# Attention: ScalarE instead of VectorE empties the bank of softmax denominators

## The chip, the cores and the metric

The kernel runs on one core of one Trainium2 chip. That core has a matrix engine (TensorE, "PE" in the profile, with its weight loads as "PEld"), VectorE ("DVE"), ScalarE ("ACT"), GpSimd ("POOL"), a queue engine for transfers ("SP"), and 16 DMA engines. The metric is the device time of one execution in microseconds (us); less is better.

## The reference, cut to what matters

The model is one image of 256 channels and 64x64 pixels. It passes a linear-attention layer on the image, then a self-attention over its 4096 pixels as tokens, then a mixture of eight experts. Only the self-attention matters here: 8 heads of 32 channels, softmax over 4096 keys, scale 256 to the power -0.5.

```python
def _L1_attn_ref(x, w_qkv, b_qkv, w_out, b_out):      # x: 1 x 4096 x 256
    qkv = x @ w_qkv + b_qkv
    q, k, v = split into 8 heads of 32
    dots = jnp.einsum('bhid,bhjd->bhij', q, k) * scale
    attn = jax.nn.softmax(dots, axis=-1)
    out = jnp.einsum('bhij,bhjd->bhid', attn, v)
    return out @ w_out + b_out
...
t = t + _L1_attn_ref(_ln_t(t), ...)
```

## The kernel before

The work is in float32. Before the loop, queries and keys lie with channels on the partitions (`qk`) and the values with tokens on the partitions (`v`). A measured bound on the scores lets the kernel leave out the subtraction of the row maximum, so each softmax is the plain exponential over its sum.

**Rounds and steps.** A round is one chunk of 512 queries (`qc`, eight of them) and one group of four heads (`g`, two of them): 16 rounds. A round has 32 steps, one for each tile of 128 keys. All 512 steps are written out in order by the list `places`, and each engine runs its own instructions in the order written, except where `tc.issue_after(x)` holds one behind instruction `x` in its engine's order.

**One step.** `scores(r, i)` multiplies 128 keys by 512 queries for four heads (L1074). Head 0 goes to the bank `one`, of which there is a single one; heads 1 to 3 go to a group of three banks, `three`, of which there are two in turn. ScalarE takes the exponential of `one` (L1082, 512 columns) and then of `three` (L1084, 1536 columns) into a weights buffer. Two steps later `value_sums` multiplies the weights by the values into the bank `acc` (L1033). So TensorE's order in the loop is: scores of step i, value products of step i - 2, scores of step i + 1, and so on.

**Denominators.** The sum of the weights over the keys is gathered in buffers: `add` (L1100, VectorE, 128x2048) adds most steps' weights to the round's total; every fourth step's are added by an accumulating DMA that GpSimd issues (L1089). At step 5 of the next round `gather` adds the two totals (L1120). At step 9 `pack` sums the total over the partitions by products with ones, into the first bank of a `three` group (`den`, L1033 again), and copies that bank to `rec` (L1129). The SP queue then writes four rows of `rec` to memory and reads them back spread over 128 partitions (L1131, L1132). At step 17 `turn` takes the reciprocal and brings it back to all channels; at step 29 `spread` multiplies the round's result (L1149). Rounds 1 to 15 do this for the round before, so `pack` runs 15 times; the last round has an ending of its own, whose copy of `acc` ScalarE makes (L1112).

**The banks around `pack`.** Since `den` takes a turn of the two `three` groups, the turns near step 9 are: step 8 the first group, step 9 the second, `den` the first, step 10 the second, step 11 the first. So step 10 waits until ScalarE has read step 9's scores, one step earlier than usual; and the scores of step 11 cannot begin until L1129 has emptied `den`. In VectorE's order L1129 stands behind an `add`.

In odd rounds from the third on, steps 13 and 25 also hold two tiles of the output projection (L1011, with VectorE's L1015 to empty it), in one `three` group.

Of the kernel before, what the change touches and what calls it, by code (L numbers as in the profile page):

```python
# [25 lines left out]
AF = mybir.ActivationFunctionType  # L26
# [5 lines left out]
C = 256  # L32
# [3 lines left out]
CH = 512  # L36
# [75 lines left out]
def tile_conv_attn_hybrid(ctx: ExitStack, tc: tile.TileContext, a: dict, out: bass.AP):  # L112
    nc = tc.nc
# [29 lines left out]
    def chunk(i):  # L143
        return slice(CH * i, CH * (i + 1))
# [41 lines left out]
    with ExitStack() as phase:  # L186
# [397 lines left out]
        def packed(jobs):  # L584

            steps = []
            for job in jobs:
                if not steps or sum(j[0] for j in steps[-1]) + job[0] > CH:
                    steps.append([])
                steps[-1].append(job)  # L590
            return steps
# [247 lines left out]
    with ExitStack() as phase:  # L839
# [179 lines left out]
        with tc.If(tame > 0) as branch:  # L1019
            with (  # L1020
# [6 lines left out]
                def three_banks():  # L1027
                    return ps.tile([P, 3, CH], F32, tag="three", name="ps_three", bufs=2)
# [26 lines left out]
                head = lambda z, hd: z[:, CH * hd : CH * (hd + 1)]  # L1055
# [1 line left out]

                rounds = [(qc, g) for qc in range(NCH) for g in range(KC)]
                places = [(r, i) for r in range(len(rounds)) for i in range(NT)]
                weights_of, acc_of, sums_of = {}, {}, {}  # L1060

                def scores(r, i):
                    qc, g = rounds[r]
                    step = NT * r + i
                    n = min(free)[1]
                    free.remove(min(free))
                    pe = buffers[n]
                    one = ps.tile([P, CH], F32, tag="one", name="ps_one")
                    three = three_banks()
                    for hd in (1, 2, 3, 0):  # L1070
                        hs = slice(D * hd, D * (hd + 1))
                        to = three[:, hd - 1] if hd else one
                        for u in range(2):
                            nc.tensor.matmul(  # L1074
                                to[CELL * u : CELL * (u + 1), :],
                                qk[hs, 1, g, P * i + CELL * u : P * i + CELL * (u + 1)],
                                qk[hs, 0, g, chunk(qc)],
                                start=True,
                                stop=True,
                                skip_group_check=True,  # L1080
                            )
                    first = nc.scalar.activation(head(pe, 0), one, AF.Exp, scale=C**-0.5)  # L1082
                    with tc.issue_after(first.ins):
                        nc.scalar.activation(pe[:, CH:], three.rearrange("p h n -> p (h n)"), AF.Exp, scale=C**-0.5)  # L1084
                    weights_of[r, i] = pe
                    if i in (own, other):
                        sums_of[r, i] = n
                    elif moved(r, i):
                        nc.gpsimd.dma_start(buffers[sums_of[r, other]], pe, accum_op=ALU.add)  # L1089
                        free.append((step + 6, n))  # L1090
                    else:
                        free.append((step + 3, n))

                def moved(r, i):
                    return i in by_dma and (r < last or i < NT - 8)
# [18 lines left out]
                def by_ones(to, weights, start, stop):  # L1114
                    per_head(to, lambda hd: ones, lambda hd: head(weights, hd), start, stop)
# [9 lines left out]
                def pack(r):  # L1125
                    den = three_banks()[:, 0]
                    by_ones(den, buffers[sums_of[r, own]], True, True)
                    rec = work.tile([P, CH], F32, tag="rec", name="rec")
                    nc.vector.tensor_copy(rec, den)  # L1129
                    some = work.tile([P, CH // D], F32, name="some")  # L1130
                    nc.sync.dma_start(dens, rec[::D, :])  # L1131
                    nc.sync.dma_start(some, packed(dens))  # L1132
                    held.append(some)
                    free.append((NT * (r + 1) + 11, sums_of[r, own]))
# [25 lines left out]
                for s, (r, i) in enumerate(places):  # L1160
                    qc, g = rounds[r]
                    scores(r, i)
                    if s > 1:
                        value_sums(*places[s - 2])
                        if places[s - 2][1] == NT - 1:
                            take(places[s - 2][0], nc.vector.tensor_copy)
                    if r and i == 5:
                        gather(r - 1)
                    if r and i == 9:
                        pack(r - 1)  # L1170
                    if r and i == 17:
                        turn()
                    if r and i == 29:
                        spread(r - 1)
                    if qc and g == KC - 1 and i in (13, 25):
                        some_projections(2)
                    if s < len(places) - 2:
                        add(r, i)

                den = three_banks()[:, 0]  # L1180
# [5 lines left out]
                rec = work.tile([P, CH], F32, tag="rec", name="rec")  # L1186
# [6 lines left out]
        with branch.Else():  # L1193


            with (
# [8 lines left out]
                for hd in range(2 * 4):  # L1205
                    g, hs = hd // 4, slice(D * (hd % 4), D * (hd % 4 + 1))
                    nc.vector.tensor_copy(ka[:D, :], qk[hs, 1, g, :])
                    for qc in range(NCH):
# [16 lines left out]
                        for i in range(NT):  # L1225
                            sc = ps.tile([P, CH], F32, tag="sc", name="ps_sc")
                            nc.tensor.matmul(sc, ka[:, tok(i)], qa, start=True, stop=True)
                            pe = work.tile([P, CH], F32, name="pe1")
# [10 lines left out]
                        rec = bigb.tile([D, CH], F32, name="rec1")  # L1239
# [10 lines left out]
    with ExitStack() as phase:  # L1250
# [15 lines left out]
        def each(name):  # L1266
            return small.tile([P, NT, NE], F32, name=name)

        def one(name):
            return small.tile([P, NT], F32, name=name)  # L1270
# [30 lines left out]
        with ExitStack() as routing:  # L1301
# [41 lines left out]
            for n in range(2):  # L1343
                first, hot, place = each(f"first{n}"), each(f"hot{n}"), one(f"place{n}")
# [295 lines left out]
```

## Time and profile before

| What | Value |
|---|---|
| median of three runs | 2819.03 us (2815.43 to 2820.85) |
| the profiled execution's own time | 2818.95 us |
| its span, first to last instruction | 2817.1 us |
| the 512 steps of attention | from 1115.6 to 2220.6 us of the span |
| TensorE busy, 1200 to 2220 us | 1011.5 of 1020 us |
| ScalarE busy, 1200 to 2220 us | 916.1 of 1020 us |
| VectorE busy, 1200 to 2220 us | 866.0 of 1020 us |
| one L1129 (VectorE, 128x512 out of a bank) | 683 ns, 15 times |
| one L1082, one L1084 (ScalarE) | 598 and 1445 ns, 512 times each |
| one L1100 (VectorE, 128x2048) | 2.29 us |

In the timeline a line gives start, duration, engine, source line, operation, and in brackets how long the engine stood idle before it and whose end released it. The ends of matrix products are modelled, so their starts are the surer figure. A step's length is best read from one L1082 to the next.

### The profile page before, as it was taken

What the parts mean: (1) busy time and instruction counts of PE and PEld (TensorE: products, weight loads), DVE (VectorE), ACT (ScalarE), POOL (GpSimd) and SP (SyncE); (2) the same over time, 40 slices, a digit from 0 to 9 for tenths busy, and PEclk for the clock granted to TensorE, in tenths of its full rate; (3) what the DMA queues carried; (4) which work ended last, traced back from release to release, by engine and by line L of the source; (5) the groups of instructions that cost most, each with busy time, mean ns of one, the idle gap of its engine ahead of it and who ended that gap; (6) DMA issues with size and microseconds to landing.
All of it is one profiled execution on the core that took longest, in us unless ns stands there. A gap on an engine that the chain in (4) does not pass through costs nothing. (4 is left out here: it accounts for less than half of the span.)

```text
span 2817.1 us, 71992 instructions
## 1 busy us (share of the span) xinstructions
PE 2668.2 (95%) x31078; PEld 1218.8 (43%) x31078; DVE 1888.8 (67%) x2491; ACT 1483.1 (53%) x2045; POOL 812.5 (29%) x914
## 2 busy tenths in 40 slices
PE   6889999988999989999999999999999689999996
PEld 5454336735434654111212121212222168888884
DVE  6758788575878886888888888888888721111114
ACT  3232323222232312999898989898988732222222
POOL 2067778205777731000000000000000022222220
PEclk9999999999999999999999999999999879999997
DMA  5000000000000000555555555555555356666665
GB/s 142 6 23 28 7 31 17 8 0 26 27 9 30 15 21 1 106 116 119 109 111 110 117 108 119 109 111 110 112 108 119 85 182 221 192 200 195 205 216 189
DMA packets 120043, 264.97 MB, mean 94 GB/s; under 512 B 20098, under 2 KB 81128, under 8 KB 105636
## 3 DMA queue, kind: packets, MB, share of 16 engines
q0 software_dynamic: 22368, 133.18, 22.2%
q1 hardware_dynamic: 90168, 118.15, 13.0%
q10 hardware_dynamic: 7180, 8.93, 0.9%
q8 instruction: 248, 4.06, 0.6%
q14 instruction: 79, 0.65, 0.1%
HBM read 126.76 MB, written 18.12 MB: 51 GB/s over the span
## 5 line engine op out<-in xcount | busy, mean ns | idle before, releaser
L1074 PE MATMUL ps_three<-qk 32*64 32x512 f32 x6144 | 566.6, 616 | 10.3 <-DVE rec L1129 7.3
L1074 PE MATMUL ps_one<-qk 32*64 32x512 f32 x2048 | 560.0, 616 | 0.6 <-ACT pe L1082 0.6
L1100 DVE TENSOR_TENSOR act<-act,pe 128x2048 f32<-128x2048 f32 x195 | 446.8, 2291 | 89.8 <-ACT pe L1084 55.2
L564 ACT COPY sm<-ps_sc 128x384 f32<-128x384 f32 (+3 forms) x454 | 218.5, 511 | 529.4 <-PE ps_sc L738 345.6
L1084 ACT ACTIVATE pe<-ps_three 128x1536 f32<-128x1536 f32 x330 | 476.9, 1445 | 0.0
L568 DVE TENSOR_TENSOR sm<-ps_sc,mask 128x512 f32<-128x512 f32 (+3 forms) x740 | 340.1, 519 | 69.9 <-PE ps_sc L738 66.8
L1100 DVE TENSOR_TENSOR act<-act 128x2048 f32<-128x2048 f32 x150 | 343.8, 2292 | 60.6 <-ACT act L1084 48.9
L568 POOL TENSOR_TENSOR sm<-sm,mask 128x192 f32<-128x192 f32 (+3 forms) x428 | 349.8, 848 | 111.9 <-ACT sm L564 111.5
L1089 POOL DMA_DIRECT2D pe<-pe x108 | 92.9, 860 | 961.7 <-ACT pe L1084 660.2
L1033 PE MATMUL ps_acc<-pe,v 128*32 128x512 f32 x2640 | 353.2, 607 | 0.0
L1549 ACT ACTIVATE hid<-ps_hp,cols 128x256 f32<-128x256 f32 (+1 forms) x288 | 133.1, 462 | 360.1 <-PE ps_hp L1546 346.3
L1074 PEld LDWEIGHTS ps_three<-qk 32*64 32x64 f32 x6144 | 113.2, 130 | 425.8 <-ACT pe L1082 232.2
L1084 ACT ACTIVATE act<-ps_three 128x1536 f32<-128x1536 f32 x182 | 263.2, 1446 | 0.0
L1546 PE MATMUL ps_hp<-xe,w 128*128 128x256 f32 (+1 forms) x1152 | 246.8, 371 | 0.0
L1555 PE MATMUL ps_yp<-w,hid 128*128 128x256 f32 x1088 | 240.8, 379 | 0.0
L1082 ACT ACTIVATE pe<-ps_one 128x512 f32<-128x512 f32 x330 | 197.3, 598 | 69.2 <-PE ps_one L1074 45.6
L738 PE MATMUL ps_sc<-qk 32*64 32x384 f32 (+3 forms) x3584 | 232.4, 458 | 0.0
L568 POOL TENSOR_TENSOR sm<-sm,ycut 128x384 f32<-128x384 f32 (+4 forms) x146 | 147.3, 1030 | 250.6 <-ACT sm L564 250.3
L1546 PEld LDWEIGHTS ps_hp<-xe,w 128*128 128x128 f32 x1152 | 201.2, 190 | 39.4 <-ACT hid L1549 5.3
L1555 PEld LDWEIGHTS ps_yp<-w,hid 128*128 128x128 f32 x1088 | 204.2, 190 | 26.4
L754 PE MATMUL ps_acc<-sm,v 128*32 128x256 f32 (+3 forms) x2688 | 213.2, 419 | 0.1
L1525 DVE TENSOR_SCALAR xe<-ps_tp,cols 128x256 f32<-128x256 f32 (+1 forms) x72 | 34.8, 525 | 239.3 <-PE ps_tp L1521 217.1
(253 smaller groups left out, 3009.8 us busy)
## 6 DMA issues: line engine op xcount, KB each, us to landing
pe<-pe POOLq DMA_DIRECT2D x108, 1024.0 KB
w<-in_L_ffn_W SPq DMA_DIRECT2D x72, 1024.0 KB
by<-recs SPq DMA_DIRECT2D x48, 256.0 KB
b<-in_L_ffn_b SPq DMA_DIRECT2D x36, 128.0 KB
rows<-in_x SPq DMA_DIRECT2D x16, 256.0 KB
zrows<-act SPq DMA_DIRECT2D x4, 1024.0 KB
y<-yrows ACTq DMA_DIRECT2D x8, 512.0 KB
y<-yrows SPq DMA_DIRECT2D x8, 512.0 KB
```

The lines of the kernel that those rows point to most:

```text
L564: nc.scalar.copy(sm[:, :used], sc[:, :used])
L568: done = engine.tensor_mul(to, of, mk.unsqueeze(1).to_broadcast(list(to.shape)))
L738: nc.tensor.matmul(scs[h][u : u + rows, at : at + n], kT[hs[h], P * i + u : P * i + u + rows], qT[hs[h], CH * ix + CELL * c0 : CH * ix + C ...
L754: nc.tensor.matmul(acc[hs[h], CELL * c0 : CELL * c1], v[:, i, hs[h]], sms[h][:, at : at + n], start=not begun[0], stop=last and at == plac ...
L1033: nc.tensor.matmul(to[D * hd : D * (hd + 1), :], lhsT(hd), rhs(hd), start=start, stop=stop, skip_group_check=True,)
L1074: nc.tensor.matmul(to[CELL * u : CELL * (u + 1), :], qk[hs, 1, g, P * i + CELL * u : P * i + CELL * (u + 1)], qk[hs, 0, g, chunk(qc)], sta ...
L1082: first = nc.scalar.activation(head(pe, 0), one, AF.Exp, scale=C**-0.5)
L1084: nc.scalar.activation(pe[:, CH:], three.rearrange("p h n -> p (h n)"), AF.Exp, scale=C**-0.5)
L1100: latest[:] = [nc.vector.tensor_add(total, total, weights_of[r, i]).ins]
L1546: nc.tensor.matmul(hp[:, :n], w1[:, k, tok(m)], x_now[:, k, :n], start=k == 0, stop=k == KC - 1)
L1549: nc.scalar.activation(hid[:, m, :n], hp[:, :n], AF.Gelu, bias=cols[:, m : m + 1])
L1555: nc.tensor.matmul(yp, hid[:, m, tok(j)], w2[:, m, :], start=m == 0, stop=m == NH - 1)
```

## The change

The copy of `den` to `rec` is made by ScalarE. A list `emptied` holds the ScalarE instruction behind which the next one has to stand. The copy is put behind L1084 of step 9, and the first exponential of step 10 is put behind the copy. Nothing else moves: the lists of instructions of TensorE, GpSimd and SP are the same in both kernels, VectorE's lacks 15 copies and ScalarE's has 15 more, each between L1084 of step 9 and L1082 of step 10. The product that first writes `den`'s bank again and the transfer of `rec` now wait for ScalarE instead of VectorE.

```diff
-                weights_of, acc_of, sums_of = {}, {}, {}
+                weights_of, acc_of, sums_of, emptied = {}, {}, {}, []
...
-                    first = nc.scalar.activation(head(pe, 0), one, AF.Exp, scale=C**-0.5)
+                    with tc.issue_after(emptied[-1]) if emptied else nullcontext():
+                        first = nc.scalar.activation(head(pe, 0), one, AF.Exp, scale=C**-0.5)
                     with tc.issue_after(first.ins):
-                        nc.scalar.activation(pe[:, CH:], three.rearrange("p h n -> p (h n)"), AF.Exp, scale=C**-0.5)
+                        emptied[:] = [
+                            nc.scalar.activation(
+                                pe[:, CH:], three.rearrange("p h n -> p (h n)"), AF.Exp, scale=C**-0.5
+                            ).ins
+                        ]
...
                     rec = work.tile([P, CH], F32, tag="rec", name="rec")
-                    nc.vector.tensor_copy(rec, den)
+                    with tc.issue_after(emptied[0]):
+                        emptied.append(nc.scalar.copy(rec, den).ins)
```

## The prediction

> **What bounds the kernel now.** I read the shares of busy time first, then the windows of the attention stage, then who waited for whom in that stage, then the timeline of one `pack`.
>
> ```profile
> 1200.00:2220.00 1020.00, 1011.52 (x11568) 211.31 (x11572) 866.04 (x500) 916.07 (x945) 87.73 (x102) 1.00 0.54 111
> ```
>
> The columns are PE, PEld, DVE, ACT, POOL, the granted clock, the DMA share and GB/s. In these 1020 us TensorE is busy for 1011.5, at full clock; ScalarE for 916 (90%), VectorE for 866 (85%). So this stage ends when TensorE is through, and only time that TensorE loses here counts. What does it lose, and to whom?
>
> ```profile
> PE ps_three L1074 <- DVE rec L1129: 7.3, 15, 0.5
> PE ps_three L1074 <- DVE t L1015: 1.2, 1, 1.2
> ```
>
> These are all the waits of TensorE in that window: 15 times some 0.5 us for the copy that the change moves, 7.3 us in all, and one 1.2 us for a projection's bank. Nothing else. Round 1's `pack` shows how one of the fifteen comes about:
>
> ```profile
> 1203.01 1.07 PE L1033 MATMUL ps_acc<-act,v 128*32 128x512 f32 x8
> 1203.78 1.45 ACT L1084 ACTIVATE pe<-ps_three 128x1536 f32<-128x1536 f32 x1
> 1203.89 1.04 PE L1033 MATMUL ps_three<-pe,ones 128*32 128x512 f32 x8
> ...
> 1204.97 2.29 DVE L1100 TENSOR_TENSOR act<-act,pe 128x2048 f32<-128x2048 f32 x1
> ...
> 1205.28 0.68 PE L1074 MATMUL ps_three<-qk 32*64 32x512 f32 x6
> ...
> 1205.81 0.59 PE L1074 MATMUL ps_one<-qk 32*64 32x512 f32 x1
> ...
> 1206.32 1.06 PE L1033 MATMUL ps_acc<-pe,v 128*32 128x512 f32 x8
> 1206.54 0.60 ACT L1082 ACTIVATE act<-ps_one 128x512 f32<-128x512 f32 x1 [1.31 <-PE ps_one L1074]
> 1207.03 1.45 ACT L1084 ACTIVATE act<-ps_three 128x1536 f32<-128x1536 f32 x1
> 1207.17 0.69 DVE L1129 COPY rec<-ps_three 128x512 f32<-128x512 f32 x1
> ...
> 1207.91 0.68 PE L1074 MATMUL ps_three<-qk 32*64 32x512 f32 x6 [0.53 <-DVE rec L1129]
> ...
> 1209.19 0.60 ACT L1082 ACTIVATE act<-ps_one 128x512 f32<-128x512 f32 x1 [0.71 <-PE ps_one L1074]
> ...
> 1211.23 0.60 ACT L1082 ACTIVATE pe<-ps_one 128x512 f32<-128x512 f32 x1
> ```
>
> L1084 at 1203.78 is step 9's. `den` is written by 1204.93 (1203.89 + 1.04), but VectorE has just begun an `add` that runs to 1207.26; the copy follows and ends at 1207.86, and step 11's scores start at 1207.91. Meanwhile ScalarE stands idle for 1.31 us ahead of step 10's first exponential at 1206.54, and 0.71 us ahead of step 11's at 1209.19. After that a step takes 2.04 us again (1209.19 to 1211.23).
>
> **The change, part by part.**
>
> *The new copy.* The nearest row is the only ScalarE copy of this form in the attention stage:
>
> ```profile
> L1112 ACT COPY act<-ps_acc x1: 586/586/586, 2223.0 to 2223.0; 128x512 f32<-128x512 f32 x1
> ```
>
> It ran behind exponentials with no table load before it; copies of 128x512 elsewhere on ScalarE take 586 to 618 ns. In the changed program's list, too, no table load is added. The copy names up to six things to wait for (the `den` products and five transfers of the round before). The transfers have long landed, and the semaphore instructions ahead of L1082 take 17 ns each, so five cost 0.09 us at most. In round 1, ScalarE is free at 1205.23, 0.30 after `den` is written. A ScalarE instruction follows the one before at a gap of 0.1 us (1203.19 to 1203.29), so the copy runs from 1205.33 to 1205.92, or 1206.05 with 618 ns and the semaphores. Step 10's exponential, tied to TensorE's products ending at 1206.40, starts at 1206.54 as before. So the copy costs nothing on the path: it is covered by the 1.31 us of idleness, with 0.5 to 0.6 to spare. Without that cover it would cost ScalarE 0.49 us (the spacing of L1082 to L1084, 1206.54 to 1207.03) to 0.59 us each time.
>
> The Trainium skill speaks against the move: "ScalarE: Activation LUTs", section "Rules for kernel authors", puts plain elementwise work on VectorE and gives ScalarE a budget of about 0.3 us + 0.83 ns per element. By that the copy would take an estimated 0.73 us instead of the row's 0.586, ending at 1206.06 at the earliest; the sum would be the same by both. For this form the trace does not agree that VectorE is the quicker: 683 ns there.
>
> *The bank is free earlier.* Instead of 1207.86 the bank is free at about 1205.92. What is late next for step 11's scores? First, TensorE's own order: the value products started at 1206.32, and scores follow value products by 0.99 to 1.00 us where nothing else waits (1200.97 to 1201.96, 1211.00 to 1212.00), giving 1207.31 to 1207.32. Second, the bank `one`, which step 10's exponential leaves at 1207.14; L1082's end releases products after 0.11 to 0.17 us, giving 1207.25 to 1207.31. Both say 1207.32 instead of 1207.91: 0.59 us, the 0.53 us of idleness and 0.06 in which groups usually overlap. ScalarE could then begin step 11 at 1207.03 + 1.55 = 1208.58, and TensorE gives it the scores at 1207.32 + 1.27 = 1208.59, instead of 1209.19: the same 0.6 us.
>
> *All rounds.* The idleness before step 11's scores is 0.53 twice, 0.52 six times, 0.50 twice, 0.45 twice, 0.40 and 0.39 twice: 7.26 us. With 15 x 0.06 = 0.90 that is 8.2 us. Counted on ScalarE, the excess of step 11 over 2.04 us (0.66 down to 0.42) sums to 8.6. I take the middle, 8.4 us. TensorE being busy 99% of this stage, what it gains early it keeps.
>
> *VectorE.* It loses 15 x 0.683 = 10.2 us of copies, worth nothing in themselves: it was not the bound. Here is a small loss to weigh. In round 1, step 10's `add` waits for L1084's data and starts at 1208.51 either way. Step 11's data then come 0.6 us earlier, at 1210.53; but the `add` ahead ends at 1210.80, so VectorE trails the steps by some 0.3 us where it used to wait 0.36 us. Every fourth step has no `add`: three adds at 2.39 us against four steps of 2.04 leave 1.0 us, which takes it back by step 13. The projection's first product to reuse that bank in round 3 starts at 1352.26, 1.2 us after L1015 ended. So I cost it at nothing, and at most 7 x 0.3 = 2 us if that slack were gone.
>
> *Queues.* SP's transfer of `rec` goes out about 1.9 us earlier; its data are needed only at step 17, 12 us later, so nothing. POOL's list is untouched; its transfers come at most 0.6 us sooner per 67 us round, and the DMA engines are at 0.54.
>
> **Sum.** 2818.95 - 8.4 = 2810.5 us for an execution like the profiled one, which stands 0.08 us below the median of the runs. Gain 0.30%.
>
> **The rivals.**
>
> *A: ScalarE is the real pacemaker (slower).* L1082 to L1084 takes 0.49 and L1084 to the next L1082 1.55, which is just the 2.04 us of a step. If ScalarE set that pace, a further copy in its order would lengthen each round and the earlier bank would give nothing back: 15 x 0.49 = +7.4 us, 2826.3. The Trainium skill's "Perfetto Trace Analysis", section "Optimizing Scalar/DVE Operations", favours handing work to ScalarE where VectorE is saturated; here the windows show VectorE at 85% and ScalarE at 90%, which speaks for this rival. Against it: after delays ScalarE runs steps of 1.93 to 1.96 us (for instance into step 16 of round 1, 1219.44), so its own limit lies below 2.04, and at `pack` it is idle for 2.0 us. It decides once copy and waits take over 0.6 us longer than the row says; the gain is eaten at some 1.2 us longer. Chance 9%.
>
> *B: the earlier bank is worth little (same).* If step 11 were held as long by something that the profile hides behind the copy (the release of `one`, a slower start of ScalarE's next instruction after a copy, VectorE trailing at the projections), half or all of the gain goes: 2814 to 2819. For it: the trace puts a wait down to the last to come. Against: both next waits were worked out above and end at 1207.3. Chance 17%.
>
> *C: the copy brings the table out (slower).* A table load in this trace takes 1.28 us; two for each copy are 2.57, less 0.6 of cover, so about 2.0 us late, of which 0.6 is gained back: 15 x 1.4 = +21, 2840. The list has no such loads. Chance 2%.
>
> *D: more than forecast.* The single 1.2 us wait for L1015 in round 15 goes too, as VectorE has less to do: 2809 and below, down to 2806 with the spread of runs. Chance 8%, counted with the forecast as faster.
>
> **How the numbers follow.** The forecast, with D, holds 72%; A and C 11%; B 17%. About 0.2% (5.6 us) is what a measurement of this kernel tells from no change, so faster means below 2813.4. The range runs from 2806 (8.6 + 1.2 of gain and 3 us of the runs' spread) to 2818 (most of B, leaving out A and C).
>
> **What the profile after would show.** A ScalarE COPY of `rec` of about 586 ns, 15 times, about 0.1 us behind step 9's L1084, and the idleness before step 10's exponential cut from 1.31 to about 0.6 us; the wait of TensorE for `rec` gone from the list of waits; step 11 at 2.04 us to 2.1 instead of 2.46 to 2.70; attention's steps ending about 8.4 us earlier. It is wrong if step 10 starts later than 3.25 us after step 9, if a new wait of step 11 for L1082 takes the old one's place, or if the steps between lengthen beyond 2.04 us.

## The result, and the profile after

The changed kernel takes 2810.6 us in the median (2806.55 to 2815.94), the kernel before, run beside it, 2817.88 us (2815.07 to 2821.07). The ratio is 0.9977, with a 95% interval of 0.9968 to 0.9985: faster by 0.23%, 6.5 us (4.2 to 9.0). (The two medians alone lie 7.3 us apart; the middle ratio over all pairs of a run of each kernel is 0.9977.) The forecast was 2810.5 us, 0.9970 of the profiled execution.

The profiled execution after has a span of 2806.9 us, 10.2 us shorter than the one before. Those 10.2 us are not the effect. From the first exponential of step 0 to that of step 32, round 0 took 69.29 us in the profile of before and 66.59 us in that of after, though the two programs do the same there: before, TensorE was granted half its clock for 13.7 us around the start of the loop (1112.7 to 1126.4, the first exponential being at 1115.6), after for 3.4 us (1120.0 to 1123.4). The traces of the experiments below fit this: in four of them no half clock falls into round 0, which then took 64.97 us each time; in three it lasted 3.4 us there, and round 0 took 66.53 or 66.54. Rounds 1 to 15, which hold the fifteen copies and run at full clock in both, are the part to compare. From the first exponential of step 32 to that of step 511 they took 1033.68 us before and 1025.32 after: 8.36 us less.

The windows of the profile after, with columns PE, PEld, DVE, ACT, POOL, granted clock, DMA share and GB/s as in the view shown of before:

```profile
1200.00:2220.00 1020.00, 1016.99 (x11604) 214.80 (x11600) 860.29 (x498) 923.95 (x961) 89.92 (x107) 1.00 0.54 111
```

TensorE is busy for 1017.0 us of 1020 instead of 1011.5. ScalarE has 8 us more to do, VectorE 6 us less (the fixed window holds some 8 us more of the program than before, so these are not just the fifteen copies). The waits of TensorE from 1200 to 2222 us:

```profile
PE ps_three L1011 <- DVE act L1196: 1.8, 2, 1.4
PE ps_three L1074 <- DVE t L1015: 1.2, 1, 1.2
```

The fifteen waits for the copy are gone. The 1.2 us for one projection's bank is still there; the 1.8 us belong to the ending of attention, which now falls into this window. Round 1's `pack` again (in this kernel L1083 is a step's first exponential, L1086 its second, L1135 the copy, L1105 an `add`):

```profile
1201.08 1.07 PE L1033 MATMUL ps_acc<-act,v 128*32 128x512 f32 x8
...
1201.86 1.45 ACT L1086 ACTIVATE pe<-ps_three 128x1536 f32<-128x1536 f32 x1
1201.97 1.04 PE L1033 MATMUL ps_three<-pe,ones 128*32 128x512 f32 x8
...
1203.04 2.29 DVE L1105 TENSOR_TENSOR act<-act,pe 128x2048 f32<-128x2048 f32 x1
1203.19 0.59 ACT L1135 COPY rec<-ps_three 128x512 f32<-128x512 f32 x1
...
1203.36 0.68 PE L1074 MATMUL ps_three<-qk 32*64 32x512 f32 x6
...
1204.40 1.06 PE L1033 MATMUL ps_acc<-pe,v 128*32 128x512 f32 x8
1204.61 0.60 ACT L1083 ACTIVATE act<-ps_one 128x512 f32<-128x512 f32 x1 [0.83 <-PE ps_one L1074]
...
1205.39 0.67 PE L1074 MATMUL ps_three<-qk 32*64 32x512 f32 x6
...
1206.58 4.69 DVE L1105 TENSOR_TENSOR act<-act 128x2048 f32<-128x2048 f32 x2 [1.25 <-ACT act L1086]
1206.66 0.60 ACT L1083 ACTIVATE act<-ps_one 128x512 f32<-128x512 f32 x1
```

VectorE is in the same `add` as before when the denominators are ready, but nobody waits for it. The copy ends at 1203.78. Step 11's scores start at 1205.39, 0.99 us after the value products at 1204.40, which is TensorE's own order; before, that distance was 1.59 us (1206.32 to 1207.91). ScalarE's idleness ahead of step 10 has gone from 1.31 to 0.83 us, and step 11 follows step 10 after 2.05 us.

### The profile page after: what moved, and what is told of

It is laid out like the page before. It is cut to its first block, busy times and chain, and to the rows that moved or that the text cites. A ratio compares the mean times of both kernels' runs of the same rounds, so it can differ in the third digit from the quotient of the medians.

```text
span 2806.9 us, 72020 instructions
## 1 busy us (share of the span) xinstructions
PE 2661.7 (95%) x31078; PEld 1217.1 (43%) x31078; DVE 1879.4 (67%) x2476; ACT 1489.9 (53%) x2060; POOL 813.6 (29%) x914
## 4 chain that ended last, share of the span: by engine, by line
PE 92%; DVE 3%; issue 2%; DMA 2%; ACT 1%; POOL 0%; SPq 0%; ACTq 0%; DVEq 0%; POOLq 0%
PE ps_three L1074 18%; PE ps_acc L1033 18%; PE ps_hp L1552 9%; PE ps_yp L1561 8%; PE ps_sc L738 8%; PE ps_acc L754 7%; PE ps_sc L641 3%; PE ps_sc L665 3%; PE ps_acc L696 3%; PE ps_mm L947 2%; PE ps_two L329 2%; PE ps_two L362 2%; PE ps_two L443 1%; PE ps_acc L684 1%; PE ps_mm L958 1%
## 5 line engine op out<-in xcount | busy, mean ns | idle before, releaser
L1105 DVE TENSOR_TENSOR act<-act,pe 128x2048 f32<-128x2048 f32 x195 | 446.8, 2292 | 97.2 <-ACT pe L1086 62.9
L1086 ACT ACTIVATE pe<-ps_three 128x1536 f32<-128x1536 f32 x330 | 476.9, 1445 | 0.0
L1105 DVE TENSOR_TENSOR act<-act 128x2048 f32<-128x2048 f32 x150 | 343.8, 2292 | 55.7 <-ACT act L1086 42.5
L1086 ACT ACTIVATE act<-ps_three 128x1536 f32<-128x1536 f32 x182 | 263.2, 1446 | 0.0
L1083 ACT ACTIVATE pe<-ps_one 128x512 f32<-128x512 f32 x330 | 197.4, 598 | 59.4 <-PE ps_one L1074 35.7
```

The costliest lines, as they stand in the source:

```text
L1105: latest[:] = [nc.vector.tensor_add(total, total, weights_of[r, i]).ins]
```

## The experiments

All of them were read in two ways: by the ratio to the kernel before, and by the length of rounds 1 to 15 in the profile, which is the sharper of the two. Every length here is the time from one step's first exponential to the next one's, and rounds 1 to 15 are from that of step 32 to that of step 511.

| Kernel | step 10, round 1 | step 11, round 1 | rounds 1 to 15 | ratio to before |
|---|---|---|---|---|
| before | 3.25 us | 2.65 us | 1033.68 us | |
| changed kernel | 3.25 | 2.05 | 1025.32 | 0.9977 (0.9968 to 0.9985) |
| VectorE, copy early | 3.25 | 2.05 | 1025.32 | 0.9961 (0.9948 to 0.9975) |
| changed, VectorE's load kept | 3.25 | 2.05 | 1025.35 | 0.9968 (0.9956 to 0.9980) |
| changed, one more copy | 3.25 | 2.05 | 1025.31 | 0.9965 (0.9952 to 0.9978) |
| changed, half the products | 3.25 | 2.05 | 1025.30 | 0.9973 (0.9962 to 0.9983) |
| changed, three more copies | 4.16 | 1.82 | 1036.55 | 1.0011 (1.0001 to 1.0020) |
| VectorE, copy later | 3.25 | 3.25 | 1043.01 | 1.0036 (1.0022 to 1.0050) |
| changed, copy behind step 10 | 3.27 | 3.26 | 1043.93 | 1.0031 (1.0020 to 1.0043) |

Five kernels in this table have the same rounds within 0.05 us and ratios from 0.9961 to 0.9977. So the differences among those ratios tell nothing.

The theory was that the gain is the earlier release of the bank, whoever makes it. The rivals were that VectorE was relieved, and that ScalarE sets the pace (rival A of the prediction).

### The copy stays on VectorE, but comes first

```diff
-                held, latest = [], []
+                held, latest, emptied = [], [], []
...
-                    nc.vector.tensor_copy(rec, den)
+                    emptied[:] = [nc.vector.tensor_copy(rec, den).ins]
...
+                    if r and i == 9:
+                        with tc.issue_after(emptied[0]):
+                            add(r, 8)
-                    if s < len(places) - 2:
+                    if s < len(places) - 2 and not (r and i == 8):
                         add(r, i)
```

> The kernel before with one order changed: the copy stays on VectorE, but the add of step 8's weights is held behind it, so that VectorE makes the copy as soon as the denominators are written. Nothing is left out. Theory (what costs is when the bank comes free, not which engine frees it): the copy starts at about 0.2 us after the denominators are written instead of 2.2 us, step 11 falls from 2.46-2.70 us to about 2.05 in all fifteen rounds, and the gain is that of the changed kernel, 8.4 us (ratio 0.997). Rival 1 (VectorE had too much to do, and the 10 us of copies taken from it are the gain): VectorE's load is that of before, so no gain, ratio 1.000. Rival 2 (VectorE falls behind by the held add and is missed at step 13): step 11 falls, but steps 12 to 15 lengthen by as much, ratio 0.999 to 1.000.

Measured: ratio 0.9961, rounds 1 to 15 at 1025.32 us, to the hundredth those of the changed kernel. Its timeline around round 1's `pack`:

```profile
1201.34 1.04 PE L1033 MATMUL ps_three<-pe,ones 128*32 128x512 f32 x8
...
1202.50 0.69 DVE L1129 COPY rec<-ps_three 128x512 f32<-128x512 f32 x1 [0.19 <-PE ps_three L1033]
...
1203.11 2.28 DVE L1100 TENSOR_TENSOR act<-act,pe 128x2048 f32<-128x2048 f32 x1
...
1203.77 1.06 PE L1033 MATMUL ps_acc<-pe,v 128*32 128x512 f32 x8
...
1204.77 0.67 PE L1074 MATMUL ps_three<-qk 32*64 32x512 f32 x6
```

VectorE waits 0.19 us for the products, copies, and only then does the `add` that stood ahead before. Step 11's scores start 1.00 us after the value products. The engine is thus not what counts: the same engine with the same work in another order gains all of it. Steps 12 to 15 did not lengthen, so rival 2 falls too (summed over the rounds they are those of before to 0.06 us).

### The changed kernel with VectorE's load put back

```diff
+                    idle = work.tile([P, 1], F32, name="idle")
+                    with tc.issue_after(latest[0]):
+                        nc.vector.tensor_reduce(idle, buffers[sums_of[r, own]][:, :CH], AX.X, ALU.max)
                     some = work.tile([P, CH // D], F32, name="some")
```

> The changed kernel with VectorE's load put back: at the old place of the copy, behind the add of step 8, VectorE reduces 128x512 of the round's total to a column that nobody uses (684 ns in the profile of before, against 683 for the copy). Nothing is left out. Theory: the same time as the changed kernel, 8.4 us below before (ratio 0.997), step 11 at 2.05 us. Rival 1 (the relief of VectorE is the gain): the time of before, ratio 1.000, with step 11 or the steps behind it long again.

Measured: ratio 0.9968; the reductions took 676 to 682 ns each, fifteen times, and rounds 1 to 15 took 1025.35 us, 0.03 more than without them. The relief of VectorE by 10 us is worth nothing.

### More copies on ScalarE: how thick is the cover?

```diff
                         emptied.append(nc.scalar.copy(rec, den).ins)
+                    for _ in range(1):                                   # 3 in the second kernel
+                        with tc.issue_after(emptied[-1]):
+                            emptied.append(nc.scalar.copy(rec, den).ins)
```

> The changed kernel with the ScalarE copy made twice, one behind the other, at the same place. Nothing is left out. Theory (ScalarE has 0.83 us of idleness left before step 10 in round 1): a second copy of some 0.6 us is covered, the idleness falls to about 0.2 us, step 10 stays at 3.25 us, and step 11 is set by the products as before: time of the changed kernel within 1 us (ratio to before 0.997). Rival A (ScalarE sets the pace): each further copy lengthens each round by 0.49 to 0.6 us, 7 to 9 us more than the changed kernel (ratio 1.000).

> The changed kernel with the ScalarE copy made four times, one behind the other. Nothing is left out. Theory: three further copies take about 1.8 us, of which 0.83 us are covered; step 10's exponential comes 1.0 us later, step 10 takes 4.2 instead of 3.25 us, fifteen times: about 15 us more than the changed kernel, 6 to 7 us over before (ratio 1.002). Rival A: 3 x 15 x 0.49 to 0.6 = 22 to 27 us more than the changed kernel (ratio 1.005 to 1.007).

Measured with one more: ratio 0.9965, rounds 1 to 15 at 1025.31 us. ScalarE in round 1, and what is left of its idleness:

```profile
1203.45 0.59 ACT L1135 COPY rec<-ps_three 128x512 f32<-128x512 f32 x1
...
1204.07 0.59 ACT L1138 COPY rec<-ps_three 128x512 f32<-128x512 f32 x1
1204.87 0.60 ACT L1083 ACTIVATE act<-ps_one 128x512 f32<-128x512 f32 x1 [0.21 <-PE ps_one L1074]
```

The idleness fell from 0.83 to 0.21 us, by the 0.62 us from one copy to the next, and the step did not move. A whole further copy is free here. With three more the cover is gone: from round 2 of that kernel,

```profile
1273.97 0.59 ACT L1135 COPY rec<-ps_three 128x512 f32<-128x512 f32 x1
...
1274.60 1.82 ACT L1138 COPY rec<-ps_three 128x512 f32<-128x512 f32 x3
...
1276.31 0.60 ACT L1083 ACTIVATE pe<-ps_one 128x512 f32<-128x512 f32 x1
...
1276.47 1.09 PE L1074 MATMUL ps_three<-qk 32*64 32x512 f32 x10 [0.22 <-ACT rec L1138]
...
1278.13 0.62 ACT L1083 ACTIVATE pe<-ps_one 128x512 f32<-128x512 f32 x1
```

Step 10 takes 4.16 us, 0.91 more, which over fifteen rounds is 13.6 us; about 1.0 us and 15 were expected. But the rounds lengthened by 11.2 us only (1025.32 to 1036.55): the next step took 1.82 us, since its scores were written before ScalarE was through with step 10 and ScalarE ran without a wait, and the one after 2.11. (The further copies read `den` too, so they also hold its bank: TensorE waited for the last of them some 0.2 us in each round, 3.3 us in all.) So a delay of ScalarE is in part made good, which neither theory said; the ratio came out at 1.0011 where 1.002 was expected. Rival A, at 22 to 27 us, is refuted by both kernels.

### The copy later on VectorE

```diff
+                    idle = work.tile([P, 1], F32, name="idle")
+                    with tc.issue_after(latest[0]):
+                        more = nc.vector.tensor_reduce(idle, buffers[sums_of[r, own]][:, :CH], AX.X, ALU.max)
+                    with tc.issue_after(more.ins):
                         nc.vector.tensor_copy(rec, den)
```

> The kernel before with the copy pushed back on VectorE: a reduction of 128x512 to a column that nobody uses (678 ns in an earlier run here) stands ahead of it, behind the add of step 8. Banks and TensorE's and ScalarE's orders in the loop are those of before. Nothing is left out. Theory (each 0.1 us by which the bank comes free later than TensorE is ready costs 0.1 us a round): the copy ends 0.78 us later, step 11 takes 3.3 to 3.45 instead of 2.46 to 2.70 us, and nothing behind it makes up for it: 15 x 0.78 = 11.7 us over before (ratio 1.004), while the early copies are held at 2.05 us by TensorE's own order. Rival (the wait has slack: other work takes its place, or VectorE makes it up by step 13): under 5 us (ratio 1.000 to 1.002).

Measured: ratio 1.0036, rounds 1 to 15 at 1043.01 us, 9.33 us over before. One reduction ahead of the copy did not cost 0.78 but 0.60 us: two neighbours on VectorE overlap.

```profile
1273.21 0.68 DVE L1131 TENSOR_REDUCE idle<-act 128x1 f32<-128x512 f32 x1
1273.81 0.68 DVE L1133 COPY rec<-ps_three 128x512 f32<-128x512 f32 x1
...
1274.54 0.68 PE L1074 MATMUL ps_three<-qk 32*64 32x512 f32 x6 [1.12 <-DVE rec L1133]
```

TensorE's wait for the copy rose from 0.53 to 1.12 us in this round, and 15 x 0.60 = 9.0 us is what the rounds show but for 0.3; these lie in round 12, where step 11 took 3.52 us, 0.95 more than before. A later release costs one for one; an earlier one gains until TensorE's own order takes over, some 0.06 us beyond the idleness that the profile names.

### The copy behind step 10's exponentials

The copy and its transfers are written one step later, and the order of TensorE's products in step 11 is pinned to that of the changed kernel (the calls alone are shown):

```diff
                     if r and i == 9:
-                        pack(r - 1)
+                        packed_now = pack(r - 1)              # den's products only
+                    if r and i == 10:
+                        pack_out(*packed_now)                 # the copy, dens, some
```

> The changed kernel with the ScalarE copy one step later in ScalarE's order: behind step 10's two exponentials instead of between steps 9 and 10. TensorE's and VectorE's orders are those of the changed kernel. Nothing is left out. Theory (the time at which the bank comes free decides; before, it was 1207.86 in round 1, in the changed kernel 0.6 us after step 9's exponentials): the copy can start only when step 10's second exponential is nearly through, 1.4 us after it starts, and ends some 2.0 us after that start, where VectorE in the kernel before ended 0.83 us after it. Step 11's products come 1.2 us later than before and 1.8 us later than in the changed kernel; ScalarE then also finds its second exponential of step 11 late. Fifteen times: 27 us more than the changed kernel, 18 us over before (ratio 1.006). Rival (what counts is which engine has the work, ScalarE or VectorE): the time of the changed kernel, ratio 0.997.

Measured: ratio 1.0031, rounds 1 to 15 at 1043.93 us. It is slower than before by 10.2 us, not by 18, and for another reason than the one expected:

```profile
1274.10 1.45 ACT L1087 ACTIVATE pe<-ps_three 128x1536 f32<-128x1536 f32 x1
1275.43 0.59 ACT L1140 COPY rec<-ps_three 128x512 f32<-128x512 f32 x1
...
1275.60 0.68 PE L1075 MATMUL ps_three<-qk 32*64 32x512 f32 x6 [1.17 <-ACT pe L1087]
```

Step 11's scores start while the copy is still running. They wait for step 10's second exponential (1274.10 + 1.45 = 1275.55) and not for the copy, which ends at 1276.02. Since there are two groups of banks, and the one that holds `den` is still being read, step 11 must have got the group that step 10 had: with the copy written after step 10, the pool no longer gave out the two in turn. So this kernel does not test what it was made for. It does show what a group used in two steps in a row costs: 3.26 us for the step instead of 2.04.

### What is left at step 10

Step 10 takes 3.25 us in both kernels, 1.21 more than a plain step. Is that the products that make the denominators?

```diff
-                    by_ones(den, buffers[sums_of[r, own]], True, True)
+                    half = buffers[sums_of[r, own]]
+                    per_head(
+                        den[:, : CH // 2],
+                        lambda hd: ones,
+                        lambda hd: half[:, CH * hd : CH * hd + CH // 2],
+                        True,
+                        True,
+                    )
...
-                        emptied.append(nc.scalar.copy(rec, den).ins)
+                        twice = den[:, : CH // 2].unsqueeze(1).to_broadcast([P, 2, CH // 2])
+                        emptied.append(nc.scalar.copy(rec.rearrange("p (t n) -> p t n", t=2), twice).ins)
```

> The changed kernel with the products that make the denominators cut to half their columns (256 of the 512 queries; the copy reads those 256 columns twice, so its length is kept). The other half of the denominators is left out. It asks what is left at step 10, which takes 3.25 us instead of 2.04 in both kernels. Theory: step 10's scores for heads 1 to 3 start 0.05 us after step 9's second exponential has emptied the other group of banks, so the turn of the banks sets them, and the products end 0.4 us before that anyway; halving them shortens step 10 by less than 0.1 us, time of the changed kernel within 1.5 us (ratio to before 0.997). Rival (the products on TensorE are the cost of step 10): 0.43 us less each time, 6.5 us below the changed kernel (ratio 0.994).

Measured: ratio 0.9973, rounds 1 to 15 at 1025.30 us, step 10 unchanged at 3.25 us.

```profile
1269.06 1.45 ACT L1086 ACTIVATE pe<-ps_three 128x1536 f32<-128x1536 f32 x1
1269.22 0.61 PE L1033 MATMUL ps_three<-act,ones 128*32 128x256 f32 x8
1269.76 1.07 PE L1074 MATMUL ps_one<-qk 32*64 32x512 f32 x2
...
1270.56 0.68 PE L1074 MATMUL ps_three<-qk 32*64 32x512 f32 x6
```

The products end 0.4 us sooner, but the scores of heads 1 to 3 still start 0.05 us behind step 9's second exponential (1269.06 + 1.45 = 1270.51). So the length of these products is not what costs. What is left at step 10 is the turn of the banks: `den` takes a turn, so step 10 gets the group that step 9 had. The parts add up to the step, in round 2 of the changed kernel: the second exponential starts 0.49 us after the first and takes 1.45, the scores follow 0.05 later, and the next first exponential 1.26 after those, 3.25 us together. It is the same cost as in the run before this one. No run here gave step 10 another group, so that the 1.2 us would go is not shown.

## Why the prediction was right, point by point

- *What bounds the stage.* Right. TensorE's waits named the 7.3 us, and what the change took away is these and the overlap beside them. The steps 11 fell from a sum of 39.22 us to 30.92: 8.30, against a forecast of 8.4 between 8.2 and 8.6.
- *What is late next.* Right in kind. Step 11's scores start 0.99 us after the value products (forecast 0.99 to 1.00), and no new wait stands in the list. The steps 11 took 2.00 to 2.11 us (forecast 2.04 to 2.1), and step 10 is later than 3.25 us only in rounds 13 to 15, by the same amount as before. The early copy on VectorE, released at 1203.19 for scores at 1204.77, shows that what limits then is not the bank.
- *The new copy.* Right that it is covered; its terms were a little off. It takes 592 ns in the median, not 586. The semaphore instructions ahead of it take 17 to 38 ns, not 17. It does not start 0.1 us behind the exponential ahead of it but 0.12 us before that one ends (1203.19 against 1201.86 + 1.45 = 1203.31). So 0.83 us of idleness were left where about 0.6 were forecast, and a whole second copy fitted in.
- *No table load.* Right: ScalarE's copies stand between exponentials at 592 ns, so rival C is out.
- *VectorE trailing by 0.3 us.* It shows, and it costs nothing, as forecast. Before, VectorE stood ready ahead of the projections' results seven times in this window, for 1.8 us; after, once, for 0.3. Steps 13 and 14 are the same to 0.02 us in every round.
- *Rival A* was refuted, and more clearly than was argued. The gap of 0.1 us that seemed to belong to ScalarE's pace is not its own: with scores at hand, ScalarE made a step of 1.82 us in the kernel with three more copies, so in a plain step of 2.04 us it waits some 0.2 us for TensorE. At 2.04 us it is not the bound, though it is 90% busy.
- *Rival B* did not come: nothing stood hidden behind the copy, as the step of 2.05 us shows. *Rival D* did not come: the wait of 1.2 us for L1015 in the last round is there in every kernel, as VectorE is as late there with less work as with more.
- *The rules weighed.* The budget that the Trainium skill's "ScalarE: Activation LUTs" gives in "Rules for kernel authors", which it states for a bias given as a pointer, 0.73 us as estimated, was above the 0.592 us measured. Its row that puts plain elementwise work on VectorE neither helped nor hurt here: left on VectorE but made first, the copy gained as much in the rounds. The Trainium skill's "Perfetto Trace Analysis", section "Optimizing Scalar/DVE Operations", also says that breaking up instructions may help where VectorE or ScalarE are not saturated but cause bubbles on other engines. The trace agrees with the diagnosis (VectorE at 85%, TensorE idle fifteen times behind one 2.29 us `add`), but turning the two instructions round was enough, and breaking up the `add` was not tried.

The time itself agreed to 0.1 us, which is luck: the median of before moved by 1.2 us between three runs and thirteen, and the gain by the ratio is known only to lie between 4.2 and 9.0 us. The 8.36 us in the rounds against the forecast 8.4 is the agreement that counts.

## What to carry to other kernels

When the busiest engine waits for a short instruction on another engine, look first at what that engine was doing when the data became ready: here a 683 ns copy stood behind a 2.29 us addition, and moving the copy ahead of it was worth as much as moving it to another engine. A high busy share did not make ScalarE the bound here; how long it stands idle right at the place of the change, and its shortest step anywhere in the trace, tell whether it can take more. Where small effects are measured, compare the stretch of the profile that the change touches, step by step, since whole executions of one kernel here differ by as much as the effect (2806.55 to 2815.94 us for the changed one).

## What was not expected

- ScalarE overlapped two neighbouring exponentials by 0.1 us and more when nothing held it: a step of two, 598 and 1445 ns, took 1.82 us in the kernel with three more copies, where the steady 2.04 us had looked like their sum.
- The pool of banks did not give out its two groups strictly in turn: writing the copy one step later changed which group step 11 got, and that cost 1.2 us a round against the changed kernel (3.26 against 2.05 us).
- Half the clock in a few stretches differs from one execution to the next at the same place in the program (13.7 us around the start of attention in one, 3.4 in another, none in a third), and moved round 0 by up to 4.3 us (69.29 to 64.97 us). What sets the length of these stretches was not tried.
